# Products of constant ones written into TensorE's order in the first stage of a four-layer kernel

## The chip, the cores and the metric

One core of a Trainium2 chip (trn2) runs the whole kernel in one launch. The metric is the device time of one execution in microseconds. Before the change the median of 3 runs is 2099.04 us (2096.14 to 2101.76).

## The reference, cut to what matters

Four blocks follow one another on an activation of 4 rows of 512 positions with 128 features (fp32). Each block adds its result to its input and normalises the sum over the features.

- **Block 1** is a gated convolution with a scan: `proj = x @ W_in.T` gives a gate and a value of 128 features each; the gate goes through a sigmoid, the value through a depthwise convolution of 5 taps; `gv = g * v`; a first-order recurrence `h = tanh(a) * h + gv` runs along the 512 positions; the result goes through `W_out` and a layer norm of its own.
- **Block 2** is a mixture of 8 experts: a router picks one expert for each of the 2048 positions, which then go through that expert's two-layer ReLU net (128 to 512 to 128) and are weighted by the gate.
- **Block 3** is causal grouped attention with rotary positions (8 query heads, 4 key heads of 128).
- **Block 4** is a six-layer local-attention transformer with 16 heads of 64, a window of 32 and a gated feed-forward net.

The change touches the code of blocks 1 and 2 alone, and computes nothing of the reference.

## The kernel before, in words

The first stage holds blocks 1 and 2. Its work is cut into named steps, each a small function that issues a few instructions. The string `STEPS` lists the names in the order in which they are issued, and `in_order` ties every instruction to the one before it on its engine. So within each engine the order of the string is the order in which the engine works, and an instruction that is not ready holds up all behind it on that engine.

Steps that the change and the prediction touch, with their lines (a digit at the end of a name is the row, the tile or the group):

- `valB` and `gateB` (L383/L388, L372) are the projections of row B, four passes over 512 columns as two records each. For row 0 the convolution is made on VectorE: `vp0` copies the value out of PSUM (ScalarE, L395), `taps0` applies the five taps (L398, L400). For rows 1 to 3 the taps are folded into five weight matrices `wc` (L824), and `valB` is five products.
- `gyB` (L406, L410) multiplies by the gate and scans; `joinB` (L419, L420) multiplies the scan's output `y` with `wout` and adds the row itself through the identity, into the tile `r`.
- `saB`, `paB`, `caB`, `naB`, `mulB`, `addB`, `sbB`, `pbB`, `cbB`, `nbB` are the two layer norms: statistics on VectorE, the power on GpSimd (L436), the affine step on ScalarE (L446), the weight on GpSimd (L466).
- `stB` stores the normalised row to DRAM (L483), `tpB` transposes it (L490), `x1TB` copies that to SBUF (L494), `lgB` makes the router's logits (L502, products of 8 columns).
- The routing of part 0 (row 0) and of part 1 (rows 1 to 3): `ch`, `cnt`, `tot`, `ends`, `pl`, `into`, `hot`, `ids`, `low`, `who`. `cnt` and `tot` (L570, L572, L586) are small bf16 products, `ids` (L648) another; `who` (L658) is the list by which `gaT` (L697) gathers the positions of a tile from DRAM.
- Per tile T of 128 sorted positions: `wT` brings the expert's first weights (a DMA from SyncE, L742, or a copy on VectorE, L747), `xstG`, `xtG` transpose a group of tiles (L706, L711), `hT` is the first layer (L754), `raT`, `rdT` its ReLU (L768, L774), `yT` the second layer (L782), `yeT` adds the bias (L788).
- `wov0`, `wov1` (L797) are products of block 3's value and output weights, which need nothing from the row work.

The stage has 8 PSUM banks: two each for the tags `mm`, `tr` and `y`, one each for `res` and `route`. `ones_h` is a 128 by 128 bf16 tile of ones (L167) which the counting products read.

After the first stage comes block 3 (the lines from L889 to L1043 in the profile) and then block 4, which takes from about 450 us to the end.

Of the kernel before, what the change touches and what calls it, by code (L numbers as in the profile page):

```python
# [16 lines left out]
P = 128  # L17
B, T, D = 4, 512, 128
NC = T // P
# [57 lines left out]


STEPS = """
val0 gate0 xin0 xin2 vp0 taps0 gate1 sig0 gy0 wc join0 sa0 pa0 val1 sig1 ca0 na0 xin1 gy1 val2  # L80
mul0 add0 sb0 join1 pb0 cb0 nb0 gate2 xin3 sa1 sig2 tp0 x1T0 pa1 gy2 lg0 gate3 st0 ca1 ch0 tot0
cnt0 ends0 pl0 na1 sig3 join2 sa2 into0 mul1 pa2 val3 ca2 hot0 na2 ids0 gy3 low0 mul2 who0 join3
add1 ga0 ga1 sb1 pb1 sa3 cb1 eid0 nb1 xst0 w1 pa3 ga2 add2 ca3 na3 w0 wov1 sb2 xt0 w2 ga3 h0
mul3 w4 xst1 wovc1 tp1 ra0 rd0 xt1 wov0 x1T1 wovc0 pb2 y0 ga4 add3 ga5 cb2 sb3 pb3 h1 nb2 lg1
tp2 ye0 ra1 rd1 y1 cb3 h2 w3 qtab x1T2 nb3 tp3 ga6 lg2 xst2 ga7 ra2 ye1 ga8 rd2 x1T3 lg3 xt2 w6
pos0 w5 ch1 y2 ga9 ye2 h3 tot1 ga10 ra3 ys1 rd3 ends1 cnt1 w7 h4 pl1 y3 ys0 ra4 xst3 rd4 h5 hot1
ra5 xt3 rd5 ye3 st2 into1 y4 y5 ye4 h6 ye5 ids1 ra6 st1 rd6 lm st3 h7 w8 low1 ra7 who1 y6 ga11
eid1 rd7 h8 ga12 y7 ra8 ye6 w9 rd8 h9 w10 ye7 exp y8 ga13 ga14 xst4 ra9 ga15 rd9 ga16 w11 xt4
h10 ga17 ye8 ra10 w12 rd10 y9 h11 ye9 w13 ga21 ra11 ga18 ga19 y10 rd11 h12 xst5 ys2 ra12 xt5
rd12 y11 ye10 ys3 h13 w14 y12 ra13 ye11 rd13 h14 ye12 ra14 w15 w16 rd14 y13 ye13 h15 ra15 ga20  # L90
xst6 ga22 w17 rd15 y14 ys4 h16 xt6 ga23 w18 br2 y15 ga24 ye14 gt0 ra16 rd16 ye15 h17 br3 ra17
br0 y16 br1 ad2 rd17 h18 ra18 w19 ga25 y17 ye16 w21 rd18 ye17 xst7 h19 ad3 ad0 y18 ra19 rd19 w20
ad1 h20 xt7 w22 ra20 ye18 w23 ga26 sp ga27 pc ys5 rd20 y19 h21 ra21 nm y20 rd21 ye19 h22 y21
ye20 w25 w24 ra22 rd22 ye21 ga28 h23 xst8 ga29 ra23 y22 xt8 rd23 h24 ra24 ye22 y23 w26 rd24 h25
ys6 ye23 y24 ra25 rd25 h26 ye24 w27 ra26 y25 w28 xst9 rd26 ye25 h27 w29 xt9 ra27 rd27 ys7 y26
ye26 h28 y27 ra28 rd28 ye27 h29 ra29 y28 rd29 y29 ye28 ye29 ys8 ys9 pos1
"""


# [34 lines left out]
def fused(ctx: ExitStack, tc: tile.TileContext, a: dict, out: bass.AP):  # L134
    nc = tc.nc
# [12 lines left out]
    def chunks(x):  # L148
        return x.rearrange("p (c d) -> p c d", c=NC)
# [16 lines left out]
    ones_h = cp.tile([P, P], BF16, name="ones_h")  # L166
# [78 lines left out]
    qtab = gwp.tile([P, 2 * T], F32, name="qtab")  # L245
# [34 lines left out]
    with ExitStack() as stage:  # L280
# [5 lines left out]
        def bank(tag, name):  # L286
            return p1.tile(
                [P, 512], F32, tag=tag, name=name, bufs=1 if tag in ("res", "route") else 2
            )
# [58 lines left out]
        wc = once.tile([P, 5, D], F32, name="wc")  # L348
# [6 lines left out]
        step = {}  # L355
# [434 lines left out]
                )  # L790


        def product(k):
            p = wov_p[k] = bank("tr", f"wov{k}")
            for i in range(4):
                h = 4 * k + i
                nc.tensor.matmul(  # L797
                    p[:, i * D : (i + 1) * D], lhsT=gwv[:, h // (NH // NKV), :], rhs=gwo[:, h, :],
                    start=True, stop=True,
                )  # L800
# [10 lines left out]
        for part, sizes in zip(parts, ((1, 2, 4, 4), (2, 4, 4, 4, 4, 1))):  # L811
            for n in sizes:
                groups.append(Group(len(groups), part, range(t, t + n)))
                for k in range(n):
                    Tile(t + k, k, groups[-1])
                t += n
        step["lm"], step["exp"], step["gt0"] = shifted, exponentials, gates
        for k in range(2):
            step[f"wov{k}"] = lambda k=k: product(k)
            step[f"wovc{k}"] = lambda k=k: product_out(k)  # L820
# [22 lines left out]
    sp = ctx.enter_context(tc.tile_pool(name="l_state", bufs=1))  # L843
# [883 lines left out]
    step = {}  # L1727
# [89 lines left out]
    step = {}  # L1817
# [187 lines left out]
```

## Time and profile before

| What | us |
|---|---|
| median of 3 runs | 2099.04 |
| the profiled execution's own time | 2115.05 |
| its span, from the first instruction to the last | 2113.2 |
| TensorE busy, whole span | 1980.1 (94%) |
| TensorE busy in 0 to 50, 50 to 100, 100 to 150 us | 34.85, 39.34, 40.99 |
| mean granted TensorE clock in the same three stretches | 0.90, 0.83, 0.97 |
| mean granted TensorE clock over the span | 0.985 |

The page divides the span into 40 equal slices and gives for each the busy share of an engine in tenths and the clock that TensorE was granted, in tenths of full speed. A view of chosen stretches gives for each engine its busy time in us and the number of its instructions, then the granted clock and the DMA engines' share and rate. The timeline gives for runs of like instructions the start, the time that they took together, and in brackets the idle time in front and what ended it. A product of fp32 operands counts as two instructions. Records of TensorE overlap, since one product is let in while the one before it drains, so the distance from start to start is what a product costs in a row of them, and not the duration of a record.

### The profile page before, as it was taken

The numbers are of one execution on the slowest core, as the hardware profiler recorded it, in microseconds if no ns is written. First come the engines' busy times: TensorE is split into PE (matmuls) and PEld (weight loads), VectorE is DVE, ScalarE is ACT, GpSimd is POOL, SyncE is SP. The second block draws the span as 40 slices with busy tenths as digits, with TensorE's granted clock in tenths as the row PEclk, the third lists the DMA queues.
The fourth block names the chain that finished last, engine by engine and source line by source line (L and its number), as shares of the span: only waits on it lengthen the run. The fifth ranks groups of instructions, "written<-read, shape, count | busy, mean of one in ns | idle before, by whom it ended". The sixth has DMA issues, their size and how long they took to land.

```text
span 2113.2 us, 80381 instructions
## 1 busy us (share of the span) xinstructions
PE 1980.1 (94%) x32980; PEld 1393.4 (66%) x32980; DVE 1615.3 (76%) x3343; ACT 1490.9 (71%) x4875; POOL 1722.8 (82%) x1388
## 2 busy tenths in 40 slices
PE   6778999999999999999999999999999999999997
PEld 4766777766566666666666666666666666666666
DVE  6447776687788887788877888778888788788874
ACT  2434344457788787888887788877887788877774
POOL 3425665589998899888999899998998999988882
PEclk9899999999999999999999999999999999999999
DMA  7530000002322224222232222232222322222221
GB/s 246 135 107 6 5 5 1 1 19 62 109 62 61 61 68 119 58 62 63 60 113 58 62 70 69 79 90 62 60 68 63 105 69 67 60 60 62 65 65 52
DMA packets 96665, 143.14 MB, mean 68 GB/s; under 512 B 17358, under 2 KB 41548, under 8 KB 95404
## 3 DMA queue, kind: packets, MB, share of 16 engines
q1 hardware_dynamic: 90828, 133.02, 23.3%
q8 instruction: 262, 4.29, 0.9%
q0 software_dynamic: 1472, 3.02, 0.7%
q10 hardware_dynamic: 4000, 1.97, 0.3%
q14 instruction: 103, 0.84, 0.1%
HBM read 36.36 MB, written 4.06 MB: 19 GB/s over the span
## 4 chain that ended last, share of the span: by engine, by line
PE 58%; DVE 14%; ACT 10%; issue 4%; DMA 3%; POOL 3%; SPq 2%; another core or an unknown queue 0%; ACTq 0%; DVEq 0%; POOLq 0%
PE q L1159 10%; PE lv L1237 6%; ACT lp L1331 6%; PE lo L1379 6%; PE ly L1403 5%; PE tp_r L210 5%; DMA vk<-vr 3%; PE ls L1303 3%; PE fa L1442 3%; PE fy L1452 3%; PE fg L1431 3%; PE gy L1028 2%; DVE lt L1182 2%; PE lpt L1356 2%; DVE fn L202 2%
## 5 line engine op out<-in xcount | busy, mean ns | idle before, releaser
L1331 ACT ACTIVATE lp<-ls,lnb,rn 128x64 f32<-128x64 f32 x1536 | 608.1, 435 | 32.2 <-DVE lnb L1321 31.9
L1192 POOL TENSOR_TENSOR ro<-lt,lt 128x512 f32<-128x512 f32 x384 | 484.4, 1275 | 54.2 <-DVE lt L1182 42.3
L1159 PE MATMUL q<-wqkvo,sA 128*128 128x512 f32 x768 | 383.2, 600 | 6.9 <-DVE sA L1411 4.4
L1178 DVE TENSOR_TENSOR lt<-q,rot 128x512 f32<-128x512 f32 x384 | 262.8, 684 | 148.6 <-ACT sq L1166 136.0
L1331 ACT ACTIVATION_READ_ACCUMULATOR lp<-ls,lnb,rn 128x1 f32 x1536 | 360.3, 235 | 0.0
L1209 POOL TENSOR_TENSOR rk<-rk,neg_half 128x16 f32<-128x16 f32 x96 | 279.0, 2906 | 52.3 <-DVE rk L1203 52.2
L1209 POOL TENSOR_TENSOR rn<-rn,neg_half 128x16 f32<-128x16 f32 x96 | 277.9, 2895 | 24.5 <-DVE rn L1203 22.0
L1166 ACT ACTIVATE sq<-q 128x512 f32<-128x512 f32 x384 | 235.3, 633 | 48.1 <-PE q L1159 28.7
L210 PEld LDWEIGHTS tp_r<-ident,ro 128*128 128x128 f32 x1536 | 183.6, 141 | 118.3 <-issue 94.5
L1182 DVE TENSOR_TENSOR lt<-q,rot 128x512 f32<-128x512 f32 x384 | 260.8, 679 | 0.0
L1195 DVE TENSOR_REDUCE ss<-sq 128x8 f32<-128x512 f32 x384 | 251.2, 674 | 2.3 <-ACT sq L1166 2.2
L1237 PE MATMUL lv<-wqkvo,sA 128*128 128x512 f32 x384 | 210.3, 630 | 23.2 <-DVE lt L1182 20.6
L1379 PE MATMUL lo<-lpT,vk 64*64 64x32 f32 x12288 | 206.0, 220 | 20.8 <-issue 19.6
L1243 ACT COPY vr<-lv 128x512 f32<-128x512 f32 x192 | 118.6, 618 | 151.2 <-PE lv L1237 98.7
L1379 PEld LDWEIGHTS lo<-lpT,vk 64*64 64x64 f32 x12288 | 192.3, 135 | 39.9 <-issue 37.9
L210 PE MATMUL tp_r<-ident,ro 128*128 128x128 f32 x1536 | 216.7, 274 | 1.6 <-ACT lpT L846 0.7
L1343 POOL TENSOR_TENSOR lp<-lp,lsum 128x512 f32<-128x512 f32 x192 | 196.5, 1045 | 9.7 <-DVE lsum L1339 9.7
L1221 POOL TENSOR_TENSOR ro<-ro,rk 128x512 f32<-128x512 f32 x192 | 196.2, 1043 | 7.4
L1159 PEld LDWEIGHTS q<-wqkvo,sA 128*128 128x128 f32 x768 | 128.7, 191 | 107.7 <-issue 45.4
L1403 PEld LDWEIGHTS ly<-oT,wqkvo 128*128 128x128 f32 x1536 | 182.2, 193 | 11.4 <-issue 10.6
L1403 PE MATMUL ly<-oT,wqkvo 128*128 128x128 f32 x1536 | 188.9, 277 | 0.3 <-ACT oT L846 0.3
L1303 PEld LDWEIGHTS ls<-kT,qT 64*32 64x32 f32 x12288 | 141.0, 105 | 43.4 <-issue 20.6
(305 smaller groups left out, 3628.8 us busy)
## 6 DMA issues: line engine op xcount, KB each, us to landing
vk<-vr SPq DMA_DIRECT2D x576, 128.0 KB
vk<-vr SPq DMA_DIRECT2D x336, 64.0 KB
wqkvo<-in_lwqkv_dram SPq DMA_DIRECT2D x6, 1536.0 KB
w<-in_ew_dram SPq DMA_DIRECT2D x20, 322.0 KB
wqkvo<-in_lwo_dram SPq DMA_DIRECT2D x6, 512.0 KB
ew<-in_ew_dram SPq DMA_DIRECT2D x8, 322.0 KB
ew<-in_ew_dram SPq DMA_DIRECT2D x8, 256.0 KB
lw<-in_lw_dram SPq DMA_DIRECT2D x6, 341.0 KB
```

The lines of the kernel that those rows point to most:

```text
L210: nc.tensor.transpose(tp[:, c * P : (c + 1) * P], i[:, c, :], ident)
L1159: nc.tensor.matmul(q, lhsT=self.xs, rhs=self.w["qkv"][:, j * 512 : (j + 1) * 512], start=True, stop=True,)
L1166: nc.scalar.activation(self.sq[j], self.q[j], AF.Square)
L1178: nc.vector.tensor_tensor(heads(t1), heads(q), cs[:, None, :].to_broadcast([P, 8, DH]), ALU.mult)
L1182: nc.vector.tensor_tensor(swapped(t2), swapped(q)[:, :, ::-1, :], sn[:, None].to_broadcast([P, 8, 2, 32]), ALU.mult,)
L1192: nc.gpsimd.tensor_tensor(self.rot[j], *self.parts.pop(j), ALU.add)
L1195: nc.vector.tensor_reduce(self.ss[:, j * 8 : j * 8 + 8], heads(self.sq[j]), AX.X, ALU.add)
L1209: nc.gpsimd.tensor_tensor(self.r[j], self.r[j], neg_half.to_broadcast([P, HEADS]), ALU.pow)
L1237: nc.tensor.matmul(v, lhsT=self.xs, rhs=self.w["qkv"][:, (4 + j) * 512 : (5 + j) * 512], start=True, stop=True,)
L1331: nc.scalar.activation(self.P[:, i, :], self.S[:, i % 2, i // 2 * KB : (i // 2 + 1) * KB], AF.Exp, bias=self.nb[:, i : i + 1], scale=self. ...
L1379: nc.tensor.matmul(self.o[to : to + DH, odd, t0 : t0 + QB], lhsT=vk[r][lo : lo + KB, s, :], rhs=self.pT[lo : lo + KB, s, r * QB : (r + 1) ...
L1403: nc.tensor.matmul(y, lhsT=self.w["o"][:, j, :], rhs=self.oT[:, j % 2, j // 2, :], start=j == 0, stop=j == INNER // P - 1,)
```

## The change: fifty-three more products, in seven places

A function `keep_warm(n)` issues `n` products of `ones_h` with itself: 128 by 128 weights and 512 moving columns (the tile repeated four times by a stride of zero), in bf16, all into one PSUM tile `idle` that takes a turn of the tag `y` and that nothing reads. Seven new steps, `warm0` to `warm6`, of 9, 18, 2, 2, 2, 8 and 12 products, stand in `STEPS`:

- `warm0` (9) ahead of all, before `val0`
- `warm1` (18) between `gate1` and `join0`
- `warm2` (2) between `tp0` and `lg0`
- `warm3` (2) and `warm4` (2) on both sides of `gate3`, between `lg0` and the counting products
- `warm5` (8) between `ids0` and `join3`
- `warm6` (12) between `wov1` and `h0`

On TensorE 53 weight loads and 53 products are added. The rest of its 6788 rows in the program keep their order. ScalarE, GpSimd and SyncE have the same instructions in the same order with the same waits. On VectorE one cast (L159, `ident_h`) stands behind all five taps of row 0 and not between them.

```diff
 STEPS = """
-val0 gate0 xin0 xin2 vp0 taps0 gate1 sig0 gy0 wc join0 sa0 pa0 val1 sig1 ca0 na0 xin1 gy1 val2
-mul0 add0 sb0 join1 pb0 cb0 nb0 gate2 xin3 sa1 sig2 tp0 x1T0 pa1 gy2 lg0 gate3 st0 ca1 ch0 tot0
-cnt0 ends0 pl0 na1 sig3 join2 sa2 into0 mul1 pa2 val3 ca2 hot0 na2 ids0 gy3 low0 mul2 who0 join3
-add1 ga0 ga1 sb1 pb1 sa3 cb1 eid0 nb1 xst0 w1 pa3 ga2 add2 ca3 na3 w0 wov1 sb2 xt0 w2 ga3 h0
+warm0 val0 gate0 xin0 xin2 vp0 taps0 gate1 warm1 sig0 gy0 wc join0 sa0 pa0 val1 sig1 ca0 na0
+xin1 gy1 val2 mul0 add0 sb0 join1 pb0 cb0 nb0 gate2 xin3 sa1 sig2 tp0 warm2 x1T0 pa1 gy2 lg0
+warm3 gate3 warm4 st0 ca1 ch0 tot0 cnt0 ends0 pl0 na1 sig3 join2 sa2 into0 mul1 pa2 val3 ca2
+hot0 na2 ids0 warm5 gy3 low0 mul2 who0 join3 add1 ga0 ga1 sb1 pb1 sa3 cb1 eid0 nb1 xst0 w1 pa3
+ga2 add2 ca3 na3 w0 wov1 warm6 sb2 xt0 w2 ga3 h0 mul3 w4 xst1 wovc1 tp1 ra0 rd0 xt1 wov0 x1T1
...
+        WARM = (9, 18, 2, 2, 2, 8, 12)
+        idle = bank("y", "idle")
+
+        def keep_warm(n):
+            for _ in range(n):
+                nc.tensor.matmul(
+                    chunks(idle), lhsT=ones_h, rhs=ones_h[:, None, :].to_broadcast([P, NC, P]),
+                    start=True, stop=True,
+                )
...
+        for i, n in enumerate(WARM):
+            step[f"warm{i}"] = lambda n=n: keep_warm(n)
```

More of the change, by code (lines that the diff above doesn't have):

```diff
@@ L79 @@
 STEPS = """
-val0 gate0 xin0 xin2 vp0 taps0 gate1 sig0 gy0 wc join0 sa0 pa0 val1 sig1 ca0 na0 xin1 gy1 val2
-mul0 add0 sb0 join1 pb0 cb0 nb0 gate2 xin3 sa1 sig2 tp0 x1T0 pa1 gy2 lg0 gate3 st0 ca1 ch0 tot0
-cnt0 ends0 pl0 na1 sig3 join2 sa2 into0 mul1 pa2 val3 ca2 hot0 na2 ids0 gy3 low0 mul2 who0 join3
-add1 ga0 ga1 sb1 pb1 sa3 cb1 eid0 nb1 xst0 w1 pa3 ga2 add2 ca3 na3 w0 wov1 sb2 xt0 w2 ga3 h0
-mul3 w4 xst1 wovc1 tp1 ra0 rd0 xt1 wov0 x1T1 wovc0 pb2 y0 ga4 add3 ga5 cb2 sb3 pb3 h1 nb2 lg1
-tp2 ye0 ra1 rd1 y1 cb3 h2 w3 qtab x1T2 nb3 tp3 ga6 lg2 xst2 ga7 ra2 ye1 ga8 rd2 x1T3 lg3 xt2 w6
@@ L86 @@
[L86 to L96, printed above, removed]
+warm0 val0 gate0 xin0 xin2 vp0 taps0 gate1 warm1 sig0 gy0 wc join0 sa0 pa0 val1 sig1 ca0 na0
@@ new lines @@
+xin1 gy1 val2 mul0 add0 sb0 join1 pb0 cb0 nb0 gate2 xin3 sa1 sig2 tp0 warm2 x1T0 pa1 gy2 lg0
+warm3 gate3 warm4 st0 ca1 ch0 tot0 cnt0 ends0 pl0 na1 sig3 join2 sa2 into0 mul1 pa2 val3 ca2
+hot0 na2 ids0 warm5 gy3 low0 mul2 who0 join3 add1 ga0 ga1 sb1 pb1 sa3 cb1 eid0 nb1 xst0 w1 pa3
+ga2 add2 ca3 na3 w0 wov1 warm6 sb2 xt0 w2 ga3 h0 mul3 w4 xst1 wovc1 tp1 ra0 rd0 xt1 wov0 x1T1
+wovc0 pb2 y0 ga4 add3 ga5 cb2 sb3 pb3 h1 nb2 lg1 tp2 ye0 ra1 rd1 y1 cb3 h2 w3 qtab x1T2 nb3 tp3
+ga6 lg2 xst2 ga7 ra2 ye1 ga8 rd2 x1T3 lg3 xt2 w6 pos0 w5 ch1 y2 ga9 ye2 h3 tot1 ga10 ra3 ys1 rd3
@@ new lines @@
+ends1 cnt1 w7 h4 pl1 y3 ys0 ra4 xst3 rd4 h5 hot1 ra5 xt3 rd5 ye3 st2 into1 y4 y5 ye4 h6 ye5 ids1
+ra6 st1 rd6 lm st3 h7 w8 low1 ra7 who1 y6 ga11 eid1 rd7 h8 ga12 y7 ra8 ye6 w9 rd8 h9 w10 ye7 exp
+y8 ga13 ga14 xst4 ra9 ga15 rd9 ga16 w11 xt4 h10 ga17 ye8 ra10 w12 rd10 y9 h11 ye9 w13 ga21 ra11
+ga18 ga19 y10 rd11 h12 xst5 ys2 ra12 xt5 rd12 y11 ye10 ys3 h13 w14 y12 ra13 ye11 rd13 h14 ye12
+ra14 w15 w16 rd14 y13 ye13 h15 ra15 ga20 xst6 ga22 w17 rd15 y14 ys4 h16 xt6 ga23 w18 br2 y15
+ga24 ye14 gt0 ra16 rd16 ye15 h17 br3 ra17 br0 y16 br1 ad2 rd17 h18 ra18 w19 ga25 y17 ye16 w21
@@ L97 @@
+rd18 ye17 xst7 h19 ad3 ad0 y18 ra19 rd19 w20 ad1 h20 xt7 w22 ra20 ye18 w23 ga26 sp ga27 pc ys5
+rd20 y19 h21 ra21 nm y20 rd21 ye19 h22 y21 ye20 w25 w24 ra22 rd22 ye21 ga28 h23 xst8 ga29 ra23
+y22 xt8 rd23 h24 ra24 ye22 y23 w26 rd24 h25 ys6 ye23 y24 ra25 rd25 h26 ye24 w27 ra26 y25 w28
+xst9 rd26 ye25 h27 w29 xt9 ra27 rd27 ys7 y26 ye26 h28 y27 ra28 rd28 ye27 h29 ra29 y28 rd29 y29
+ye28 ye29 ys8 ys9 pos1
 """
```

## The prediction

> **What bounds the kernel now.** I read the page's slices first, then the granted clock in stretches of the first 75 us, then TensorE's timeline there, then its waits. The first view, the page's slices of 53 us:
>
> ```profile
> PE   6778999999999999999999999999999999999997
> ...
> PEclk9899999999999999999999999999999999999999
> ```
>
> TensorE is full from slice 5 on; in slices 1 to 4 it is not, and its clock is below full too. Only this head can be moved by the change. Stretches of 3.41 us, laid on the instants at which the clock changes (columns: length, busy us of PE, PEld, DVE, ACT, POOL, granted clock, DMA share, GB/s):
>
> ```profile
> 10.22:13.63 3.41, 0.29 (x1) 0.00 (x0) 3.20 (x6) 0.60 (x1) 0.00 (x0) 1.00 1.01 293
> 13.64:17.05 3.41, 2.39 (x11) 2.39 (x12) 2.71 (x2) 0.00 (x0) 1.93 (x1) 0.50 1.10 349
> 17.05:20.46 3.41, 3.41 (x10) 2.20 (x10) 1.33 (x9) 0.00 (x0) 0.53 (x1) 0.50 1.10 342
> ...
> 30.70:34.11 3.41, 2.16 (x12) 1.35 (x12) 2.36 (x11) 2.56 (x6) 1.02 (x1) 1.00 1.01 409
> 34.12:37.53 3.41, 3.41 (x18) 2.11 (x18) 2.64 (x10) 2.11 (x5) 1.08 (x1) 0.50 1.07 317
> 44.36:47.77 3.41, 1.56 (x14) 1.59 (x15) 3.38 (x11) 0.00 (x0) 1.97 (x2) 1.00 0.00 0
> ...
> 51.18:54.59 3.41, 0.84 (x7) 0.84 (x8) 2.59 (x12) 3.10 (x10) 2.90 (x4) 1.00 0.52 110
> 54.60:58.01 3.41, 2.52 (x13) 2.10 (x13) 2.96 (x13) 1.71 (x5) 2.75 (x3) 0.50 0.87 228
> 58.01:61.42 3.41, 3.41 (x18) 3.41 (x18) 0.29 (x1) 2.27 (x6) 3.11 (x3) 0.50 1.20 324
> ...
> 64.84:68.25 3.41, 2.84 (x20) 1.95 (x18) 0.29 (x1) 2.63 (x9) 1.56 (x2) 1.00 0.24 40
> 68.25:71.66 3.41, 2.88 (x15) 2.77 (x14) 1.69 (x6) 1.07 (x3) 0.00 (x0) 0.50 0.38 109
> ```
>
> The clock has two values. It halves after a stretch with little done (0.29 or 0.84 us of 3.41), stays full after 1.56 us, and comes back after a stretch that was full. It also halves after 30.70 to 34.11, busy 2.16 us, and after 64.84 to 68.25, busy 2.84 us: those hold transposes (L490) and 8-column products (L502), which seem to count for little. The timeline shows the price and the gaps:
>
> ```profile
> 7.04 3.47 PE L372 MATMUL gate<-xT,win 128*128 128x512 f32 x4
> ...
> 14.66 0.79 PE L419 MATMUL r<-wout,y 128*128 128x128 f32 x2 [4.16 <-DVE y L410]
> ...
> 38.82 4.46 PE L388 MATMUL val<-xT,wc 128*128 128x512 f32 x10
> ...
> 46.21 0.46 PE L419 MATMUL r<-wout,y 128*128 128x128 f32 x2 [2.85 <-DVE who L658]
> ...
> 53.75 1.33 PE L754 MATMUL h<-xt,w 128*128 128x128 f32 x8 [2.59 <-ACT xt L711]
> ...
> 59.02 1.92 PE L782 MATMUL y<-ew,hT 128*128 x8
> ...
> 63.24 1.06 PE L782 MATMUL y<-ew,hT 128*128 x8
> ```
>
> A 512-column fp32 record costs 0.43 us at full clock (ten from 38.82 to 43.12) and 0.87 in the first 10 us (four in 3.47), where the page still prints 1.00: nothing was recorded before 10.22, the durations say half. The gaps, 4.16, 2.85 and 2.59 us, wait for VectorE and ScalarE, which get no work from this change.
>
> **Price of an added product.** The trace has no 512-column bf16 product. The nearest row is the 128-column one of L953: the next product starts 0.05 us behind it at full clock (169.23 to 169.28) and 0.10 at half (160.96 to 161.06). Four times that is about 0.22 and 0.43 us. The fp32 record of 512 columns bounds it from above, 0.43 and 0.87; the 8-column bf16 products of L586 and L572, several in 0.2 us (36.17 to 36.43 holds eight, 0.03 each), bound it from below. I take 0.22 and 0.43, the same type. Its weight load (L586 on the same tile, 0.10 us) lies beside the product before.
>
> **Part by part**, against the profiled execution's own time of 2115.05 us (span 2113.2).
>
> *warm0 (9).* The ones are written by 1.11 us and `val0` waits for its DMA until 5.20. Nine at half clock take 3.9 us, from about 1.2 to 5.1: they fit, at no cost while that DMA covers them. Real work follows at once, so a full stretch is complete somewhere from 4.6 to 8.0 us, depending on where the free-running stretch begins, and not at 10.22. `val0` at full clock would save 0.85 us; over those phases the mean is 0.4. That is on the path, since `vp0` and the taps wait for it: **-0.4** (0 to -0.85).
>
> *warm1 (18).* 18 by 0.22 is 3.9 us in a gap of 4.16: free, hidden by row 0's taps and scan. The clock then stays full where it fell at 13.64. `join0` took 3.58 us (14.66 to 18.24); the same eight pairs of row 1 take 1.79 (27.93 to 29.72): **-1.8**. `val1` and `val2` took 9.69 us together against 2 by 4.30: 1.1 saved in `val1`: so `gy1`, which starts at 23.92 when `val1` ends, comes 3.3 earlier. Next late is `mul0` (GpSimd, ends 25.10), which follows `join0` by 2.2, to 22.9: `add0` moves from 26.10 to about 22.9: **-1.0** for val1. The loads for row 2 were issued by 5.98 us and are no limit.
>
> *warm2, 3, 4 (6).* Two in the gap of 0.67 ahead of `lg0`, 0.43 us: free. Between `lg0`'s end and `cnt`'s start (34.3 to 36.17) lie `gate3`, 1.85 at half, and now 0.93 plus four at 0.22, 1.8: even. `join2` behind takes 1.8 instead of 2.4, `val3` ends so much earlier, and `gy3` and `who0` with it: **-0.6**. Were the clock still half, the four would cost up to 1.7.
>
> *warm5 (8).* 1.7 us in the gap of 2.85 (behind it is `join3`, which waits for the scan): **0**, with 0.4 us of margin left even at 0.31 each.
>
> *warm6 (12).* 2.6 us in the gap of 2.59 ahead of `h0`: **+0.1**, up to +2.6 at half clock; I put **+0.2** for phases in which the clock has dropped before. It fills 51.18 to 54.59 (0.84 busy), so the halving at 54.60 goes. Saved: `tp1` 0.4, `wov0` 0.8, `y0` 0.8 (59.02 to 60.73 against 63.24 to 64.14), `h1` and `h0` 0.4: 2.4; the copies and norms on ScalarE between (nb2 at 59.75) keep about 0.3: **-2.1**. Tile 1's weights were issued at 52.06 on SyncE and are not waited for at 60.73; 2.4 us less slack is still some.
>
> The VectorE cast of 0.21 us moves within the same chain: 0. The tile `idle` takes a bank that `y1` gets next, on the same engine: 0.
>
> Sum: -0.4 -1.8 -1.0 -0.6 +0.1 +0.2 -2.1 = **-5.6 us**, to 2109.4 in the profiled execution's terms. That execution lies 16.0 above the median; I carry the difference over: 2099.04 - 5.6 = 2093.4, which is 0.27% faster. What follows (second routing, gathers, expert tiles, blocks 3 and 4) starts from these steps and has no event tied to absolute time, so it shifts whole.
>
> **A rule weighed.** The row: 30.70 to 34.11 was busy 2.16 of 3.41 us, and the clock halved. The Trainium skill, page "TensorE: Matmul & The Clock Gate", section "What's actually happening", has the clock halve after an idle window of about 3.4 us. The window's length agrees with this trace (3.41); "idle" does not, 63% busy was not enough. By the rule alone warm2 to warm4 would have nothing to prevent, and the sum would be -5.0 instead of -5.6.
>
> **Rivals.**
>
> *More than forecast.* The clock also fell at 68.25 for 6.8 us, in which TensorE was busy 5.9. Where the shifted work meets the free-running stretches otherwise, that halving goes too: another 3.0, so 2099.04 - 8.6 = 2090.4. For it: the dip follows one stretch of transposes and small products. Against: nothing was added there.
>
> *Lost downstream.* Between 91 and 120 us TensorE waits 3.45 and 4.84 us for ScalarE (L768), whose own releaser the trace doesn't name; if these are tied to something that doesn't move, or one more appears, the gain is gone: 2099.0 (2097 to 2102). Against: GpSimd's gathers there follow `who1`, which moves.
>
> *Slower: the added products run at half clock and hold up real work.* They are always ready, real products are not, and TensorE keeps its order. At 0.43 each: warm1 7.7 in 4.16 (+3.6), warm2 +0.2, warm3 and 4 +1.7, warm5 3.4 in 2.85 (+0.6), warm6 5.2 in 2.59 (+2.6): +8.7, 2107.7. It passes +6.3 (0.3%) when three quarters of them run so, with nothing gained. For it: warm6 has no slack. Against: 10.22 to 13.63 had full clock without any added product. The Trainium skill's same page, section "Measured speedup vs the span model", says that matmuls are strict FIFO without reordering; this trace agrees, TensorE sat 4.16 us at `join0`, and no later product went ahead.
>
> **How the numbers follow.** Forecast 0.58, gain 3.5 to 8 us around 5.6. About 0.3%, 6.3 us, is what a measurement here tells from no change, and the forecast lies across it: 0.27 beyond, 0.31 within. More 0.20 (all faster); lost downstream 0.13 (0.11 within, 0.02 slower); held up 0.09 (slower). Faster 0.47, same 0.42, slower 0.11. The likeliest case's own range is 2091 to 2095.5. With the other cases, the two ends of the unknown costs (each burst free or at half clock) and the spread of the runs shown (5.6 us), 2087 to 2102 leaves out most of the held-up case and the far end of more, 0.15.
>
> **What the profile will show.** Right: 53 records of L799; those of warm1 some 0.22 apart; granted clock 1.00 from 8 to about 60 us; `join0` starting near 14.3 and lasting 1.8; `add0` near 23; the second list (L658, 83.41) near 78. Wrong: L799 at 0.43 after 10 us; `join0` or `h0` waiting with no gap ahead; a half-clock stretch on `wov0` and `y0` all the same; or `who1` early and the wait at 91 to 120 us longer by as much.

## The result, and the profile after

The kernel with the added products takes 2093.68 us (median of 9 runs, 2086.94 to 2095.62), against 2098.26 us (9 runs, 2090.11 to 2101.89) for the kernel before on the same chip. The ratio is 0.9974 with a 95% interval from 0.9962 to 0.9987, which is 5.5 us less (2.7 to 8.0): a small gain, inside what was forecast. A second measurement, in a later set of runs, gave 0.9965 (0.9951 to 0.9980).

The profiled execution takes 2094.51 us with a span of 2092.6 us. That it lies 20.5 us below the profiled execution of before is not the effect: a second profiled execution of the kernel before, taken later, took 2092.43 us. What was odd was the first one: it spent 65.9 us between the second list (L658, 83.41) and the first transpose of block 3 (L210, 149.28), where the second spent 49.3 (78.97 to 128.31).

In the page's slices of the kernel after, of 52 us each, TensorE's first four slices went from 6, 7, 7, 8 tenths to 8, 9, 8, 9, in part by the added products themselves:

```profile
PE   8989999999999999999999999999999999999997
...
PEclk9999999999999999999999999999999999999999
```

The groups of instructions show 53 added products, which take 15.4 us of TensorE. A record lasts 0.44 us; the next one starts 0.22 us behind it, so the records overlap:

```profile
L799 PE MATMUL idle<-ones_h 128*128 128x512 bf16 x53 | 15.4, 440 | 1.2 <-DVE vp L353 1.2
```

TensorE's timeline of the kernel after (start, time together, instructions, idle time in front and what ended it):

```profile
1.17 4.02 PE L799 MATMUL idle<-ones_h 128*128 128x512 bf16 x9 [1.17 <-DVE vp L353]
5.50 1.72 PE L384 MATMUL val<-xT,win 128*128 128x512 f32 x2 [0.31 <-DMA xT<-in_xT_dram]
...
8.86 4.04 PE L799 MATMUL idle<-ones_h 128*128 128x512 bf16 x18
15.69 0.49 PE L420 MATMUL r<-wout,y 128*128 128x128 f32 x2 [2.79 <-DVE y L411]
...
34.06 1.01 PE L799 MATMUL idle<-ones_h 128*128 128x512 bf16 x2
...
36.58 1.05 PE L799 MATMUL idle<-ones_h 128*128 128x512 bf16 x2
...
51.54 2.75 PE L799 MATMUL idle<-ones_h 128*128 128x512 bf16 x12
54.29 1.16 PE L755 MATMUL h<-xt,w 128*128 128x128 f32 x8
...
58.35 1.13 PE L783 MATMUL y<-ew,hT 128*128 x8
```

The nine products of `warm0` end before the DMA that `val0` waits for. The eighteen of `warm1` take 4.04 us, 0.22 each, inside the wait of `join0`. But `join0` starts at 15.69 and not near 14.3, and the stretches of 3.41 us of the same kernel (columns as before: length, busy us of PE, PEld, DVE, ACT, POOL, granted clock, DMA share, GB/s) show that the clock fell twice all the same:

```profile
13.59:17.00 3.41, 1.31 (x11) 1.31 (x12) 2.76 (x2) 0.00 (x0) 0.96 (x1) 1.00 1.08 358
17.00:20.41 3.41, 3.41 (x10) 2.11 (x9) 1.33 (x9) 0.00 (x0) 0.63 (x1) 0.50 1.09 340
...
30.65:34.06 3.41, 2.66 (x14) 1.58 (x15) 2.36 (x10) 2.44 (x6) 1.02 (x1) 1.00 1.03 428
34.07:37.48 3.41, 3.41 (x9) 1.27 (x9) 1.64 (x8) 2.10 (x5) 1.20 (x1) 0.50 1.07 388
```

The half-clock stretch of before from 54.60 to 61.42 is gone (`y0`, 1.92 us at 59.02 before, takes 1.13 at 58.35), and so is the one from 68.25. So this one trace says: nothing gained up to `add0` (25.95 against 26.10), all of it from 50 us on. That was my first reading, and the experiments take it apart.

### The profile page after: what moved, and what is told of

It reads as the page before. It is cut to its first block, busy times and chain, and to the rows that moved or that the text cites. A ratio compares the mean times of both kernels' runs of the same rounds, so it can differ in the third digit from the quotient of the medians.

```text
span 2092.6 us, 80391 instructions
## 1 busy us (share of the span) xinstructions
PE 1980.7 (95%) x32937; PEld 1390.2 (66%) x33033; DVE 1613.1 (77%) x3343; ACT 1487.9 (71%) x4875; POOL 1723.3 (82%) x1388
## 3 DMA queue, kind: packets, MB, share of 16 engines
q10 hardware_dynamic: 4000, 1.97, 0.3%
## 4 chain that ended last, share of the span: by engine, by line
PE 58%; DVE 14%; ACT 12%; POOL 6%; DMA 4%; issue 4%; SPq 2%; ACTq 0%; DVEq 0%; POOLq 0%
PE q L1173 9%; ACT lp L1345 6%; PE lv L1251 6%; PE lo L1393 5%; PE ly L1417 5%; PE tp_r L211 4%; DMA vk<-vr 4%; PE fa L1456 3%; PE fg L1445 3%; PE ls L1317 3%; PE fy L1466 3%; PE gy L1042 2%; DVE lt L1196 2%; PE lpt L1370 2%; DVE lt L1192 2%
## 5 line engine op out<-in xcount | busy, mean ns | idle before, releaser
L1345 ACT ACTIVATION_READ_ACCUMULATOR lp<-ls,lnb,rn 128x1 f32 x1536 | 366.2, 238 | 0.0
```

The costliest lines, as they stand in the source:

```text
L1345: nc.scalar.activation(self.P[:, i, :], self.S[:, i % 2, i // 2 * KB : (i // 2 + 1) * KB], AF.Exp, bias=self.nb[:, i : i + 1], scale=self. ...
```

## The experiments

Each kernel has its own profiled execution, and the ratios are against the kernel before on the same chip. The edits are of the one tuple `WARM`, unless a diff says otherwise; a kernel with fewer products computes the same outputs.

### What each kernel gave

The starts of four steps, in us: `join0`, `add0` (VectorE), `who0` (the first list), and the first transpose of block 3.

| kernel | `WARM` | ratio (95% interval) | `join0` | `add0` | `who0` | block 3 |
|---|---|---|---|---|---|---|
| before | none | 1 | 14.66 | 26.10 | 45.99 | 149.28 |
| before_again | none | one run, 2092.43 us | 15.01 | 26.13 | 47.61 | 128.31 |
| e_small | all, 8 columns | 0.9994 (0.9981 to 1.0007) | 16.27 | 27.36 | 48.84 | 129.41 |
| e_late | 0 0 0 0 0 8 12 | 0.9993 (0.9981 to 1.0006) | 16.00 | 27.44 | 48.55 | 129.27 |
| e_w234 | 0 0 2 2 2 0 0 | 0.9996 (0.9983 to 1.0008) | 15.64 | 27.07 | 48.85 | 131.65 |
| e_w0 | 9 0 0 0 0 0 0 | 1.0014 (1.0002 to 1.0027) | 14.23 | 25.67 | 47.01 | 130.99 |
| e_xin2_alone | none, `xin2` moved | 1.0011 (1.0001 to 1.0021) | 15.00 | 26.44 | 47.45 | 128.89 |
| after | 9 18 2 2 2 8 12 | 0.9974 (0.9962 to 0.9987) | 15.69 | 25.95 | 46.54 | 126.70 |
| after_again | 9 18 2 2 2 8 12 | 0.9965 (0.9951 to 0.9980) | 14.27 | 23.85 | 42.58 | 125.48 |
| e_early | 9 18 2 2 2 0 0 | 0.9975 (0.9961 to 0.9989) | 14.09 | 23.67 | 45.83 | 127.13 |
| e_w01 | 9 18 0 0 0 0 0 | 0.9971 (0.9960 to 0.9982) | 14.17 | 23.75 | 46.32 | 129.97 |
| e_no6 | 9 18 2 2 2 8 0 | 0.9987 (0.9976 to 0.9999) | 14.35 | 23.93 | 45.66 | 126.79 |
| e_xin2 | 9 18 2 2 2 8 12, `xin2` moved | 0.9965 (0.9951 to 0.9978) | 13.90 | 23.46 | 44.00 | 124.56 |
| e_early_xin2 | 9 18 2 2 2 0 0, `xin2` moved | 0.9969 (0.9960 to 0.9978) | 14.71 | 24.28 | 46.20 | 128.06 |

The upper seven have no eighteen wide products ahead of `join0`, and none is measurably faster; e_w0 and e_xin2_alone lie just above 1, by about 0.1%, and nothing here explains that. The lower seven have them, and all are faster.

A mean granted clock was taken of every execution, not only of the profiled one. Averaged over a set of executions it is 0.984 in each of the three later sets of the kernel before, 0.988 to 0.991 in the seven sets with the eighteen products, and 0.983 to 0.986 in e_small, e_w234, e_w0 and e_xin2_alone. So the mean clock is higher in every set that shows the gain. That alone is not enough: e_late has 0.988 too, and no gain that can be told.

### The kernel before once more, and the products without their work

> The kernel before, unchanged, for a second trace of it. The profiled execution shown of before took 2115.05 us, 16 above the median of its unprofiled runs; between 83 and 149 us it has waits of 3.45 and 4.84 us whose releaser the trace doesn't name, and the step from the second list (L658) to the transposes of block 3 (L210) took 65.9 us, against 49.5 after the change. Theory 1 (those waits are a chance of that one execution): here the step takes 50 to 58 us and the execution 2095 to 2103. Theory 2 (they belong to the kernel before, and the change removes them): the step takes 64 us or more again, and a profiled execution some 2115. Both expect half-clock stretches at about 14 to 20, 34 to 38 and 55 to 62 us.

It took 2092.43 us, with 49.3 us in the step that was named, both slightly below what the first theory expected and far from the second. The 16.0 us by which the first profiled execution lay above the median did not come back: with them fall its waits of 3.45 and 4.84 us between 91 and 120 us, which one rival built on. What held it up there stays open.

```diff
-                    chunks(idle), lhsT=ones_h, rhs=ones_h[:, None, :].to_broadcast([P, NC, P]),
+                    idle[:, 0:8], lhsT=ones_h, rhs=ones_h[:, 0:8],
```

> All 53 added products at their places, but each of 8 moving columns in place of 512, so that TensorE has almost nothing to do in them. They leave out nothing of the reference. Theory 1 (the change acts by keeping the clock up): the half-clock stretches of before come back (14 to 20, 34 to 38, 55 to 62 us) and the ratio is 1.000, 0.9985 to 1.0015. Rival (it acts by what is moved: the PSUM bank's turn, the place of the cast, the instruction stream): the ratio stays at 0.9974.

0.9994 (0.9981 to 1.0007). TensorE's timeline of this kernel:

```profile
10.24 0.59 PE L799 MATMUL idle<-ones_h 128*128 128x8 bf16 x18
16.27 0.79 PE L420 MATMUL r<-wout,y 128*128 128x128 f32 x2 [5.43 <-DVE y L411]
```

The same 53 products, with the same order of instructions and the same moved cast on VectorE, but with 0.59 us of work where there were 4.04: the clock is half at `join0` (0.79 against 0.49), as it is from 12.7 to 19.5, 36.6 to 43.4 and 50.2 to 60.5 us, and the gain is gone. So what the change earns, it earns by TensorE's time being filled; neither the moved cast nor the new order earns it. (The traces put the cast ahead of the last of row 0's five taps, at 11.53 us in the kernel after, and not behind all five.)

### The late half and the early half

```diff
-        WARM = (9, 18, 2, 2, 2, 8, 12)
+        WARM = (0, 0, 0, 0, 0, 8, 12)
```

> Only the last two bursts (8 behind the ids, 12 ahead of the first expert tile); the other 33 products are gone. Theory 1 (most of the gain is made between 50 and 68 us, as the two traces show: the first list at 45.99 before and 46.54 after, the choice of part 1 at 72.25 and 67.78): ratio 0.9975, 0.996 to 0.999, no half-clock stretch at 55 to 62 us. Rival, the prediction's own split (3.6 us of the gain made by the first five bursts, 2.0 by the last two): ratio 0.999.

0.9993 (0.9981 to 1.0006): the half in which the first trace seemed to win everything gives nothing that can be measured, although the trace shows full clock from 42.1 to 62 us.

```diff
-        WARM = (9, 18, 2, 2, 2, 8, 12)
+        WARM = (9, 18, 2, 2, 2, 0, 0)
```

> Only the first five bursts (9, 18, 2, 2, 2); the 20 products behind the ids and ahead of the first expert tile are gone. Theory 1 (the early bursts bring nothing to the first list's time, since the scan's end came 1 us later and the clock fell at 17 us in the trace after): ratio 1.000, 0.999 to 1.0015. Rival, the prediction's split: about 3.6 us, ratio 0.9983, with the first addition of row 0 (L469 there) near 23 us in place of 26.

0.9975 (0.9961 to 0.9989): the other half gives as much as all seven. TensorE's timeline of this kernel:

```profile
8.94 4.05 PE L799 MATMUL idle<-ones_h 128*128 128x512 bf16 x18
14.09 0.49 PE L420 MATMUL r<-wout,y 128*128 128x128 f32 x2 [1.10 <-DVE y L411]
...
15.98 8.77 PE L389 MATMUL val<-xT,wc 128*128 128x512 f32 x20
```

`join0` runs at full clock and lasts 1.89 us (14.09 to 15.98), where before it took 3.58, and the 20 records behind it start 2.26 us earlier. The first reading is refuted: the products that make the gain are those ahead of `join0`, in the first 15 us. The kernel after's own profiled execution shows almost nothing of it up to `add0`, although its 2094.51 us lie only 0.8 above the median.

### The kernel after once more

> The changed kernel, unchanged, for a second trace and for times beside the next three on one chip. Both theories expect a ratio of 0.9975 to the kernel before. Theory 2 (below) expects the half-clock stretches of the head at other places than in the first trace (17.0 to 20.4 and 34.1 to 37.5 us there).

0.9965 (0.9951 to 0.9980). This execution has what the forecast described, `join0` at 14.27 lasting 1.89 and full clock up to 46.80. Then the twelve of `warm6` meet a clock that has just fallen. Stretches, and TensorE's timeline of the same kernel:

```profile
43.39:46.80 3.41, 1.45 (x13) 1.25 (x12) 3.31 (x19) 0.00 (x0) 2.90 (x4) 1.00 0.08 17
46.80:50.21 3.41, 2.58 (x11) 2.22 (x12) 1.71 (x8) 2.15 (x6) 3.17 (x3) 0.50 0.18 22
```

```profile
32.42 1.02 PE L373 MATMUL gate<-xT,win 128*128 128x512 f32 x2
...
47.63 0.48 PE L707 MATMUL xst<-ident,xs 128*128 128x128 f32 x1 [2.80 <-DMA xs<-x,who]
...
49.61 4.75 PE L799 MATMUL idle<-ones_h 128*128 128x512 bf16 x12
54.20 1.05 PE L755 MATMUL h<-xt,w 128*128 128x128 f32 x8
```

The twelve take 4.75 us instead of 2.75, and `h0` follows the first transpose of its group by 6.57 us (47.63 to 54.20), against 3.82 in the kernel after (50.47 to 54.29) and 3.81 before (49.94 to 53.75). That is 2.8 us, about the upper bound that the forecast had put on `warm6`; of the 2.8 us by which that transpose was ahead of the kernel after's, 0.1 is left at `h0`.

### Which products are needed

```diff
-        WARM = (9, 18, 2, 2, 2, 8, 12)
+        WARM = (9, 18, 0, 0, 0, 0, 0)
```

> Only the first two bursts (9 ahead of val0 and 18 ahead of join0). Theory 1 (the whole gain is row 0's head: val0, join0 and val1 at full clock, some 3.2 us by the prediction's sum): ratio 0.9975 as with all seven, the first addition (L470 there) near 23 us where nothing delays the scan. Rival (two, two and two products around the logits matter as well, 0.6 us by the sum): 0.9985 here and 0.9995 with those three alone.

0.9971 (0.9960 to 0.9982): `warm0` and `warm1` alone carry the gain.

```diff
-        WARM = (9, 18, 2, 2, 2, 8, 12)
+        WARM = (0, 0, 2, 2, 2, 0, 0)
```

> Only the three bursts of two around the logits of row 0. Theory 1: they bring nothing, since at half clock they hold up the counting products by 1.3 us (36.17 before, 37.43 after) and do not keep the clock up; ratio 1.000 to 1.001. Rival (the prediction's term of 0.6 us): 0.9995, with full clock from 34 to 38 us.

0.9996 (0.9983 to 1.0008), which is -0.8 us with an interval from -3.6 to +1.7: the six products around `lg0` and `gate3` give nothing that can be measured, and the -0.6 of the forecast is too small to be told from 0 here. What the traces do show is the clock. With these products it fell between 30 and 35 us in six of seven traces all the same. The one without that dip is after_again, where a stretch that ended at 33.15 held 0.73 us of `gate3` (which starts at 32.42, above) besides the products.

```diff
-        WARM = (9, 18, 2, 2, 2, 8, 12)
+        WARM = (9, 0, 0, 0, 0, 0, 0)
```

> Only the first burst of 9. Theory 1 (val0 alone gains 0.4 to 0.9 us from it, and the clock falls again in the gap ahead of join0): ratio 0.9997, 0.9985 to 1.0005, val0 near 1.1 us in its record and a half-clock stretch over join0. Rival (the first burst is what counts, since the scan starts earlier): 0.9975, as with all.

1.0014 (1.0002 to 1.0027). TensorE's timeline of this kernel:

```profile
5.50 1.25 PE L384 MATMUL val<-xT,win 128*128 128x512 f32 x2 [0.32 <-DMA xT<-in_xT_dram]
...
14.23 0.80 PE L420 MATMUL r<-wout,y 128*128 128x128 f32 x2 [5.21 <-DVE y L411]
```

`warm0` does what it was to do, `val0` runs almost wholly at full clock (1.25 us for its two records, 2.05 before, 1.10 at best, in e_early), but TensorE then waits 5.21 us, the clock falls at 12.7, and `join0` is slow as before. The ratio lies above the 0.9985 to 1.0005 that had been expected. So `warm0` alone earns nothing; whether `warm1` needs it wasn't tried.

```diff
-        WARM = (9, 18, 2, 2, 2, 8, 12)
+        WARM = (9, 18, 2, 2, 2, 8, 0)
```

> The changed kernel without its last burst (the 12 products ahead of the first expert tile). In the second trace of after those 12 ran at half clock (49.61 to about 54.1 us, 4.75 with the drain) and the first expert tile started at 54.20, 6.6 us behind its transposes in place of 3.8; in the first trace they ran at full clock and cost nothing. Theory 1 (the burst takes back in some executions what it brings in others): ratio as with it or up to 0.0010 lower, 0.9960 to 0.9975 where after is 0.9970. Rival (the prediction's term of 2.0 us for that burst): the ratio rises by 0.0010 to about 0.9980.

0.9987 (0.9976 to 0.9999), against 0.9974 and 0.9965 with all seven and 0.9975 for e_early, which has neither `warm5` nor `warm6`. It is higher than both values that had been expected (at most 0.9975, or 0.9980 if the burst's forecast term holds), but all these intervals overlap; what `warm6` is worth in time is not settled.

### The row that GpSimd adds

In the kernel after's profiled execution `join0` was late for a reason of its own. VectorE's and GpSimd's timelines of that kernel:

```profile
13.30 2.33 DVE L411 TENSOR_TENSOR_SCAN y<-decay,g 128x512 f32<-128x512 f32 x1
```

```profile
13.29 1.26 POOL L464 TENSOR_TENSOR sA<-sA,row 128x512 f32<-128x512 f32 x1 [3.01 <-DMA sA<-in_x_dram]
```

The scan that `join0` waits for took 2.33 us. It starts 0.01 us behind an addition on GpSimd (`xin2`, which nobody needs until `add2`), and ends at 15.63, 1.08 us behind the end of that. TensorE waited 2.79 us there, so only 1.31 us of the stretch up to 17.00 were busy, and the clock fell. To take away the meeting, `xin2` is moved behind `pa0`:

```diff
-warm0 val0 gate0 xin0 xin2 vp0 taps0 gate1 warm1 sig0 gy0 wc join0 sa0 pa0 val1 sig1 ca0 na0
+warm0 val0 gate0 xin0 vp0 taps0 gate1 warm1 sig0 gy0 wc join0 sa0 pa0 xin2 val1 sig1 ca0 na0
```

> The changed kernel with one step moved: GpSimd's addition for row 2 (xin2) stands behind the first power (pa0) and not at the head. In the traces of after, of the small products and of the late bursts that addition ran at 12.9 to 13.3 us and row 0's gate product or scan on VectorE took 1.67 to 2.33 us in place of 0.75 and 1.22, ending when GpSimd ended. Theory 2 (that meeting of GpSimd and VectorE holds the scan up by 1 us in some executions and, by lengthening the gap ahead of join0, lets the clock fall): the scan takes 1.22 us, join0 starts before 14.5 us, no half-clock stretch at 14 to 21, ratio 0.9965. Rival (the scan was held up by something else): scan again above 1.6 in its trace or join0 after 15, ratio as after.

0.9965 (0.9951 to 0.9978), as much as after_again, which was measured beside it. VectorE's timeline of this kernel:

```profile
12.62 1.22 DVE L411 TENSOR_TENSOR_SCAN y<-decay,g 128x512 f32<-128x512 f32 x1
13.76 0.80 DVE L838 TENSOR_TENSOR wc<-win,row 128x640 f32<-128x640 f32 x1
```

The scan takes 1.22 us, and the `wc` product behind it 0.80 (1.82 in after_again, where `xin2` lies beside it); `join0` starts at 13.90, the earliest of all, and the clock stays full until 32.0. So the meeting was the cause in that trace. It goes otherwise in other executions: in after_again the scan began first (12.99 against 13.14) and took 1.23 us. That moving the addition does not show in the median would fit this, but is not shown.

> No added products at all, only GpSimd's addition for row 2 behind the first power. What the meeting with VectorE is worth by itself. Theory 2: 1 us in the executions in which the two meet on the gate product or the scan (four of the nine traces so far), so 0.4 to 1 us on the mean, ratio 0.9997, 0.9985 to 1.0005; join0 at half clock as before. Rival (the meeting also costs beyond it, through the clock): 0.9985 or less.

The move without any product gives 1.0011 (1.0001 to 1.0021): by itself it earns nothing; a gain of 0.4 to 1 us had been expected.

> The first five bursts alone, with GpSimd's addition for row 2 behind the first power: the two findings together, without the bursts that can run at half clock ahead of ready work. Theory: the lowest of all, ratio 0.9955 to 0.9965. Rival (the gain beyond some 5 us is taken back downstream, at the gathers): 0.9970 as after.

0.9969 (0.9960 to 0.9978), a median of 2089.99 us (11 runs) against 2096.76 for the kernel before on that chip. It beats the kernel before, but the lower ratio that had been expected, 0.9955 to 0.9965, did not come; against the kernel after (0.9974 and 0.9965) no difference can be told.

## Why the prediction was right, step by step

The time came out as forecast (2093.4 against 2093.68), the direction and the mechanism too: without work in the products there is no gain. The sum's single terms did less well, and that they add up to within 0.3 us of the measured time is luck.

**The free products.** The price was right: 0.22 us at full clock and 0.43 at half, which is also what the products show (18 in 4.04 us; two in 0.85, from 36.58 to 37.43). `warm0`, `warm1` and `warm5` fit into their waits.

**warm0, -0.4.** Right in kind: with the nine products `val0` takes 1.10 to 1.97 us, against 2.04 to 2.05 without. The spread is what the forecast meant by its 0 to -0.85. By itself it is worth nothing that can be measured (e_w0).

**warm1, `join0` -1.8.** This is the heart of it, and right: `join0` lasts 1.89 us in six of the seven traces with the eighteen products (2.40 in the kernel after's own) and 3.4 to 3.6 in the seven without, 1.6 less on the means.

**warm1, `val1` -1.0.** This step failed. `add0` was to come 3.2 us earlier, near 22.9; it came at 23.46 to 24.28 in six traces, 2.5 earlier on the means of seven and seven (24.13 against 26.60). Of these 2.5 us, 0.8 come from an earlier start of `join0` (in part because GpSimd's addition held VectorE up in three of the upper seven), 1.6 from its duration and 0.1 from what follows. VectorE's and then GpSimd's timelines of the kernel before, first execution:

```profile
24.71 1.47 DVE L410 TENSOR_TENSOR_SCAN y<-decay,g 128x512 f32<-128x512 f32 x1
26.10 0.66 DVE L469 TENSOR_TENSOR xA<-xA,sA 128x512 f32<-128x512 f32 x1
```

```profile
23.83 1.27 POOL L466 TENSOR_TENSOR xA<-xA,row 128x512 f32<-128x512 f32 x1 [1.64 <-ACT xA L446]
```

The same of after_again:

```profile
21.54 1.23 DVE L411 TENSOR_TENSOR_SCAN y<-decay,g 128x512 f32<-128x512 f32 x1
...
23.85 0.69 DVE L470 TENSOR_TENSOR xA<-xA,sA 128x512 f32<-128x512 f32 x1 [1.09 <-POOL xA L467]
```

```profile
21.70 2.11 POOL L467 TENSOR_TENSOR xA<-xA,row 128x512 f32<-128x512 f32 x1 [1.63 <-ACT xA L447]
```

`gy1` did come earlier, with `val1`, and `mul0` starts where the forecast had it. But the scan now begins ahead of `mul0` on GpSimd, which then takes 2.11 us instead of 1.27, and `add0` waits for `mul0`; in the first execution of before `mul0` began first, and the scan was the one held up (1.47 instead of 1.22) and the last. The forecast had let `mul0` keep its 1.27 us. So `add0` follows the end of `join0` by 7.7 us where it followed by 7.8: of the saving in `val1` 0.1 us is left on the path, and not 1.0. Two traces without the wide products show the same by chance: in before_again and e_small `val1` and `val2` ran at full clock behind a slow `join0` (8.75 us instead of 9.86), `mul0` took 2.10, and `add0` came 7.68 us behind the end of `join0`.

**warm2 to warm4, -0.6.** The step failed, whatever its size in time. The clock halved there in six of seven traces, and in the kernel after two of the three pairs ran at half clock and held up `cnt0`, which stood at 37.43, 1.3 us later than before. The forecast had seen that transposes and 8-column products seem to count for little, and still took six products as enough, without a row that shows how many are. A stretch with 2.66 us (30.65 to 34.06, with two of the products) was not enough, nor one with 3.00 in e_xin2 (28.55 to 31.96, with four, the last in part): what they held besides was mostly transposes (1.48) and 8-column products. Where the clock stayed up, in after_again, `who0` follows `add0` by 18.7 us, against 19.9 to 22.6 in the other thirteen traces. So there was something to gain, in one trace, and what failed is keeping the clock up with so few. The Trainium skill, page "TensorE: Matmul & The Clock Gate", section "Part 4: PE-mode transpose", says that transposes do not count as TensorE's work in the same way; these stretches agree. The rule that was weighed, that an idle stretch halves the clock, would have given 0 for these six products. The measured time cannot tell that from -0.6, but its reason does not fit, since the stretch was 78% busy.

**warm6, +0.1 + 0.2 and -2.1.** In part. With full clock in front it fits and costs nothing (51.54 to 54.29), and `y0` follows `h0` by 4.0 to 4.2 us in three traces with `warm6` (3.0 in after_again, where `h0` is late), against 4.9 on the mean of the ten without wide products there: most of the -0.4 and -0.8 for `tp1` and `wov0`. The +2.6 at half clock came about in after_again (2.8 us more). In time the -2.1 is neither shown nor refuted: e_late has -1.5 us with an interval from -4.0 to +1.3.

**The sum.** `warm0` and `warm1` were to give -3.2 of the -5.6, and e_w01 has -6.1 us (0.9971 of 2098.13; -8.4 to -3.8). So the total was right while its parts were not: the two early bursts gave all of it and the late ones nothing that can be told. In the traces I can follow only half: on the means, `add0` and `who0` are 2.5 us earlier, the second list 2.9 (77.26 against 80.17), and block 3 starts 2.8 us earlier (126.96 of seven with the eighteen products against 129.75 of six without; for the list and for block 3 the first execution of before is left out). The starts of block 3 scatter by 1.3 and 1.8 us within each group, so this difference is uncertain by about 1.8, and what follows to the end scatters between 1961.7 and 1971.0 us. Single executions show no clear link either: before_again, with `add0` at 26.13, took 2092.43 us, and e_w01's profiled execution, with `add0` at 23.75, took 2100.25, the slowest of its ten. Where the remaining 2 to 4 us come from stays open.

**The difference carried over.** It was right to work against the profiled execution's own time and to carry its 16.0 us over: the odd 65.9 us lay behind the steps that the sum speaks of. The second list at 77.25, near the 78 that was named, proves little, since it stood at 78.97 in before_again without any product.

**The rivals.** Lost downstream: not seen, block 3 starts earlier by as much as `add0`. Held up at half clock: its mechanism is real in two places (`warm3` and `warm4` in the kernel after, `warm6` in after_again), but far from the three quarters at which it decides. The strict order of matmuls, on which this rival rests, is stated by the Trainium skill, page "TensorE: Matmul & The Clock Gate", in the section "The mechanism" of Part 3, and not in the one that the prediction names. More than forecast: 0.9965 in after_again is -7.3 us, between the two; the half-clock stretch at 68.25 that it counted on is gone in the kernel after, but there is none in 62 to 75 us of e_late either, without any gain.

**What the profile was to show.** The 53 records and the 0.22 us came. The full clock from 8 to about 60 us came in no trace: its first fall was at 17.0 us in the kernel after, at 46.8 in after_again and at 29.8 to 32.0 in the other five with the eighteen products. One sign of being wrong came too, products at 0.43 us behind 10 us, in `warm3` and `warm4` of the kernel after.

## What to carry to other kernels

Work that keeps a clock up pays where a long wait is followed at once by dense work on the critical path (4 us of products ahead of 1.9 us of `join0`), and must fill nearly the whole wait (0.5 to 1.4 us left open kept the clock up, 2.8 did not); two products here and there among transposes did not keep the clock up, and a burst that starts after the clock has fallen costs up to twice its price, in front of what it was to help. Price the saving only up to the next engine: a step that comes earlier may now run beside another engine's, and take the saving back. And take two profiled executions before explaining a few microseconds, since one trace here put the gain into the wrong half of the stage.

## What the runs showed of the hardware

- VectorE and GpSimd held each other up. The same scan took 1.22 us alone and 2.33 when GpSimd's addition of the same size had begun 0.01 us before; where VectorE came first, GpSimd's operation grew, from 1.27 to 2.11. The one held up ended 1.04 to 1.08 us behind the end of the other. The Trainium skill, page "SBUF — State Buffer", section "SBUF: two separate sides", has the two engines share one pair of ports, which a VectorE operation with two inputs in SBUF and a GpSimd operation that reads SBUF hold for a whole instruction; the durations agree nearly, as 1.04 to 1.08 us is a little less than the 1.22 to 1.27 that the operations take alone.
- The granted clock stayed full after a stretch of 3.41 us with 1.56 us of TensorE's work (before, 44.36 to 47.77) and fell after one with 1.45 (after_again, 43.39 to 46.80); both held the products of `join3`. After stretches that were mostly transposes and 8-column products it fell with 2.66 us (after, 30.65 to 34.06) and with 3.00 (e_xin2, 28.55 to 31.96), so busy time alone doesn't decide it.
- The same kernel's first fall of the clock, once it was up, came at 17.00 us in one profiled execution and at 46.80 in another.
